# Layer 3 of a four-layer convolution and attention kernel: gate chain moved by a slot, two copies moved to ScalarE, copy order changed, lead-in rearranged

## The chip, the cores and the metric

The kernel runs on one core of a Trainium2 chip. The core has a matrix engine (PE in the profile; the loading of its stationary operand is the row PEld), a vector engine (DVE, VectorE), an activation engine (ACT, ScalarE), a general engine (POOL, GpSimd) and an engine that only issues DMAs and waits (SP, SyncE). Each engine works through its own list of instructions in order; where one needs what another makes, it waits on a semaphore. The metric is device time in microseconds of one execution; lower is better. Three executions of the kernel before took 3566.73, 3568.6 and 3573.8 us; their median, 3568.6, is the time before.

## What is computed

The input is 4 images of 256 channels and 48 x 48 pixels, f32. Four layers follow, each of the form `x = x + layer(gn(x))`, where `gn` is a group norm over groups of 8 channels. Layer 0 is attention with 8 heads, layer 1 a set of depthwise convolutions that make a gate, layer 2 attention with one head of 64 channels and a batch norm behind it, layer 3 a channel gate, a 3 x 3 depthwise convolution and an instance norm. The change touches the end of layer 2 and layer 3:

```python
def _L2_conv_ref(...):                       # x: 4 x 256 x 48 x 48, normalised
    ...
    y = jnp.einsum('bnm,bmc->bnc', attn, g_x)
    y = y.transpose(0, 2, 1).reshape(b, -1, h, w)
    wy = jnp.einsum('oc,bchw->bohw', W_w, y) + W_b[:, None, None]
    mean = wy.mean(axis=(0, 2, 3))
    var = wy.var(axis=(0, 2, 3))
    out = bn_gamma[:, None, None] * (wy - mean[:, None, None]) * jax.lax.rsqrt(var[:, None, None] + EPS) + bn_beta[:, None, None]
    return out

def _L3_conv_ref(x, attn_w1, attn_w2, refine_w, refine_b):
    ...
    p = jnp.mean(xw, axis=(2, 3))
    h = jax.nn.leaky_relu(p @ attn_w1.T, SLOPE)
    a = jax.nn.sigmoid(h @ attn_w2.T)
    y = xw * a[:, :, None, None]
    y = jax.lax.conv_general_dilated(y, refine_w, window_strides=(1, 1), padding='SAME', feature_group_count=C, dimension_numbers=('NCHW', 'OIHW', 'NCHW'))
    y = y + refine_b[None, :, None, None]
    mu = jnp.mean(y, axis=(2, 3), keepdims=True)
    var = jnp.mean(jnp.square(y - mu), axis=(2, 3), keepdims=True)
    y = (y - mu) * jax.lax.rsqrt(var + EPS)
    return jax.nn.leaky_relu(y, SLOPE)
```

The batch norm of layer 2 takes its mean and variance over all four images, so layer 3 can start only when the last image's attention is done.

## The kernel before

Layers 0 to 2 are one long stream in which attention slots are filled with the projections, norms and gates of other images. A table of jobs (`fills`, `due`) says in which slot each job is put into the engines' lists. The last phase is layer 2's attention of image 3: 27 slots, three units of 9. When a unit ends, `last` (line 429) schedules its denominator (`total_here`), the sum and division on VectorE (`fold`, `divide`) and `note`, two reductions of the denominator that feed a check of the number range.

Behind the attention come `sample_means` (bn_aggr for each image), `w_stats` of the last third of image 3 (line 1341: the product with W_w and bn_stats of it), and then layer 3's lead-in, lines 1405 to 1743: the batch norm's scale `sc2` and shift `bi2`, the images' means, the first products `first` and `ahead`, and for tiles 0 and 1 the steps `grow`, `border`, `spread_out` and `square`.

Layer 3 works on 8 tiles: image (in the order 1, 2, 3, 0) by half of the channels. Tile i has its padded picture in one of four buffers `pads` (50 x 50). `grow` (line 1457, VectorE) writes x plus layer 2's output into the picture, `border` (POOL) its rim. The depthwise convolution runs on PE. For this the picture is copied into `shifted`, a buffer with four sections j, each holding 32 channels' picture at up to three positions q of the partitions, shifted by one column. These copies are made by `spread_out(i, h)` for each half h of the picture: 12 copies of 32 x 1298 f32, of which 8 change partitions (q != j) and 4 don't. The 8 are DMAs on SP's queue. The 4 are POOL copies for h = 0 and DMAs on SP's queue for h = 1. There are three `shifted` buffers, used in turn.

The steady part is a table `events` of time slots (lines 1746 to 1812). A slot is one sixth of a tile: 12 matmuls (24 passes) of the convolution. Tile i starts at slot t = 6 i. In a slot the jobs are put out by rank: FRONT, CONV, PRODUCT, GROW, EVICT, SMALL, MOMENTS, SQUARE, SCALE, LAST, PLACE, STORE. So each engine's order is fixed by slot and then by rank; within one rank, by the order in which the jobs were entered, tile by tile. The jobs of a tile that starts at t:

- the picture is made at t-9 to t-7: W_w product on PE (PRODUCT, one PSUM tile `w` for all), `grow` on DVE, `border` at t-9; squares of it on ACT at t-8 to t-6; `spread_out` at t-6 (h = 0) and t-3 (h = 1)
- convolution at t to t+5; eviction and squares of the result on ACT at t+2 to t+7
- `moments` and `scales` on DVE at FRONT of t+8, with a power on POOL; `shift` on DVE at LAST of t+8
- normalising: `scale` on ACT at t+9 to t+11, `leak` and `gain` on DVE (LAST) at t+10 to t+12, `store` (DMA on SP) at t+11 to t+13.

For every second tile, that is for every image, the gate chain runs (class `Chain`, line 1513): `total` (DVE), `groups` (PE), `inverse` (DVE, POOL), `pooled` (DVE), `first_layer` (PE), `hidden` (DVE), `second_layer` (PE), `gate` (ACT), `scaled` (DVE). Its products land in free columns of the PSUM tile of the slot in which they are put out, `now["ps"]`. It is entered at t+1, each DVE or ACT step at FRONT of its slot and each PE step at SMALL. Twelve slots, two tiles, are one image's period. A similar chain of one matmul, `judge`, is entered at slot 8.

Of the kernel before, what the change touches and what calls it, by code (L numbers as in the profile page):

```python
# [78 lines left out]
def usual_path(  # L79
# [333 lines left out]

    due, fills = {}, {}

# [13 lines left out]
    def last(u, t):  # L429

        take(u)
        if u.get("soon"):
            todo = [
                (fills, 1, lambda: total_here(u)), (due, 2, lambda: fold(u, nc.vector)),
                (due, 2, lambda: divide(u, nc.vector)), (due, 2, lambda: note(u)),
            ]
            after = 3
        else:
            todo = [
                (fills, AT_TOTAL, lambda: total(u)), (due, AT_FOLD, lambda: fold(u, nc.gpsimd)),  # L440
                (due, AT_INVERT, lambda: invert(u)),
                (due, AT_DIVIDE, lambda: divide(u, nc.gpsimd)),
            ]
            after = AT_AFTER
        todo += [(fills, after, fn) for fn in u["after"]]
        for when, dt, fn in todo:
            when.setdefault(t + dt, []).append(fn)
# [623 lines left out]

    def w_mul(b, k, c):

        ab = [pj_tile()[:, :SL] for _ in range(2)]
        for i, cc in enumerate(HALVES):
            for r, out in zip(HALVES, ab):
                c0 = k * P + i * D
                nc.tensor.matmul(
                    out[cc], lhsT=Ww[r, c0 : c0 + D],
                    rhs=y_of(b)[r, c * SL : (c + 1) * SL], start=True, stop=True,  # L1080
                )
        return [(c, ab[0]), (c + L2C, ab[1])]

    def w_stats(b, k, c):
        for s, ps in w_mul(b, k, c):
            nc.vector.bn_stats(bst[:, k, b * NSL + s, :], ps)

    def l2_unit(b, c, s2):
        return {
            "pt": {}, "qc": slice(c * SL, (c + 1) * SL), "of": s2, "after": [],  # L1090
            "paired": PAIRED if b == B - 1 else range(NG), "scale": D ** -0.5,
            "soon": b == B - 1,
            "o": lambda: y_of(b)[:, c * SL : (c + 1) * SL],
        }
# [200 lines left out]
    for b in range(B):  # L1295
# [21 lines left out]
        else:  # L1317
            spread(work, stats(b, 0), [16, 17])
            spread(work, stats(b, 1), [23, 24])
            others.append((tap_matrices(), 1 + len(SHIFT), 4, 22))  # L1320
        phases.append(([l2_unit(b, c, twos[b]) for c in range(L2C)], work, others))
# [16 lines left out]
    attend(phases)  # L1338
    for b in range(NX):
        sample_means(b)  # L1340
    for k in range(NK):
        w_stats(B - 1, k, L2C - 1)
    strict.close()
# [60 lines left out]

    for sh in shifted:
        nc.gpsimd.memset(sh[0:32, 2:4, :], 0.0)
    first = [w_product(0, c, cv_tile()) for c in range(L2C)]
    ahead = [w_product(1, 0, w_tile())]

    mv2 = lp.tile([P, NK, 2], F32, name="mv2")  # L1410
    for k in range(NK):
        nc.vector.bn_aggr(mv2[:, k, :], bst[:, k].rearrange("p s f -> p (s f)"))
    sc2 = lp.tile([P, NK], F32, name="sc2")
    var2 = lp.tile([P, NK], F32, name="var2")
    nc.vector.tensor_scalar(var2, mv2[:, :, 1], BN_EPS, None, ALU.add)
    rsqrt(sc2, var2)
    bi2 = lp.tile([P, NK], F32, name="bi2")
    nc.vector.tensor_add(bi2, mv2[:, :, 0], vec[:, V_WB, :])
    nc.vector.tensor_sub(bi2, vec[:, V_WB, :], bi2)
    sample_means(B - 1)  # L1420
    nc.vector.tensor_mul(sc2, sc2, vec[:, V_G2, :])
# [15 lines left out]

    of_groups = columns_of(first[0], B * NK)
    nc.tensor.matmul(
# [16 lines left out]

    def grow(i, c, ps):

        n, k = TILES[i]
        xs = XT[SEQ[n]][:, k, :].rearrange("p (h r c) -> p h r c", h=2, c=HW)  # L1460
        to = inside(i, c)
        for h in range(2):
            nc.vector.scalar_tensor_tensor(
                to[:, h], ps[:, h, :SL].rearrange("p (r c) -> p r c", c=HW),
                sc2[:, k : k + 1], xs[:, h, c * RS : (c + 1) * RS, :], ALU.mult, ALU.add,
            )
# [28 lines left out]

    def place(i, h, j, q, eng):
        to = shifted[(2 * i + h) % 3][32 * q : 32 * q + 32, j, :CL]
        c0 = h * HB * W2 + SHIFT[j, q]
        fr = pads[i % 4][32 * j : 32 * j + 32, c0 : c0 + CL]
        if eng is nc.gpsimd:  # L1500
            eng.tensor_copy(to, fr)
        else:
            eng.dma_start(to, fr)

    def spread_out(i, h, own=None):

        for j, q in SHIFT:
            if q != j:
                place(i, h, j, q, nc.sync)
        for j in range(4):  # L1510
            place(i, h, j, j, own or (nc.sync if h else nc.gpsimd))

    class Chain:
# [5 lines left out]
        def steps(self):  # L1519
            of, b = {}, self.b  # L1520

            def total(_):
                of["sq"] = sq = small.tile([P, NK], F32, tag="gn_sq", name="gn_sq")
# [4 lines left out]

            def groups(ps):
                of["ps"] = ps[:, 0:NK]  # L1530
                nc.tensor.matmul(of["ps"], lhsT=gmat, rhs=of["sq"], start=True, stop=True)

            def inverse(_):
                gv = small.tile([P, NK], F32, tag="gn_gv", name="gn_gv")
                nc.vector.tensor_scalar(gv, of["ps"], GN_EPS, None, ALU.add)
                of["rs"] = small.tile([P, NK], F32, tag="gn_rs", name="gn_rs", bufs=6)
                rsqrt(of["rs"], gv)

            def pooled(_):
                of["pm"] = pm = small.tile([P, NK], F32, tag="pm", name="pm")  # L1540
                nc.vector.tensor_mul(pm, dev[:, b, :], of["rs"])

            def first_layer(ps):
                of["ps"] = ps[0:D, 0:1]
                for k in range(NK):
# [4 lines left out]

            def hidden(_):
                raw = small.tile([D, 1], F32, tag="hraw", name="hraw")
                nc.vector.tensor_copy(raw, of["ps"])
                of["hl"] = hl = small.tile([D, 1], F32, tag="hl", name="hl")
                nc.vector.scalar_tensor_tensor(hl, raw, SLOPE, raw, ALU.mult, ALU.max)

            def second_layer(ps):
                of["ps"] = ps[:, 0:NK]
                for k in range(NK):
                    nc.tensor.matmul(  # L1560
                        ps[:, k : k + 1], lhsT=w2[:, k * P : (k + 1) * P], rhs=of["hl"],
                        start=True, stop=True,
                    )

            def gate(_):
                of["ga"] = small.tile([P, NK], F32, tag="ga", name="ga")
                nc.scalar.activation(of["ga"], of["ps"], AF.Exp, scale=-1.0)

            def scaled(_):
                ga = of["ga"]  # L1570
# [6 lines left out]

            return [
                (total, groups), (inverse, None), (pooled, first_layer), (hidden, second_layer),
                (gate, scaled),  # L1580
            ]
# [122 lines left out]
    def judge():  # L1704

        of = {}

        def lows(_):
            ok = lp.tile([P, 2, LW], F32, name="ok")
# [4 lines left out]

        def count(ps):
            of["ps"] = ps[0:1, 0:1]
            nc.tensor.matmul(of["ps"], lhsT=of["okm"], rhs=ones[:, 0:1], start=True, stop=True)

        def compare(_):
            nc.vector.tensor_scalar(sound, of["ps"], P - 0.5, None, ALU.is_ge)  # L1720

        return [(lows, count), (compare, None)]

# [3 lines left out]

    grow(0, 0, first[0])
    edges()
    border(0)  # L1730
    for c in range(1, L2C):
        grow(0, c, first[c])
    for h in range(2):
        spread_out(0, h, nc.scalar)
    centres()
# [9 lines left out]

    FRONT, CONV, PRODUCT, GROW, EVICT, SMALL, MOMENTS, SQUARE, SCALE, LAST, PLACE, STORE = range(12)
    events = {}
# [6 lines left out]
    def put_chain(t, parts):  # L1754
        for dt, (head, tail) in enumerate(parts):
            at(t + dt, FRONT, lambda fn=head: fn(None))
            if tail:
                at(t + dt, SMALL, lambda fn=tail: fn(now["ps"]))

# [13 lines left out]
    def put_tile(t, cv, final):  # L1773
# [11 lines left out]
        at(t + 8, FRONT, cv.scales)  # L1785
        at(t + 8, LAST, cv.shift)
        for g in range(NG3):
            at(t + 9 + g, SCALE, lambda g=g: cv.scale(g))
            at(t + 10 + g, LAST, lambda g=g: cv.leak(g))
            at(t + 10 + g, LAST, lambda g=g: cv.gain(g))  # L1790
            at(t + 11 + g, STORE, lambda g=g: cv.store(g))

    def reload(k):
        nc.sync.dma_start(XT[0][:, k, :], x_out[:, k, :])

    for i, cv in enumerate(convs):
        t = i * NSL
# [6 lines left out]
        if i % NK == 0:  # L1804
            put_chain(t + 1, chains[i // NK].steps())
        if i < NK:
            at(t + 14, STORE, lambda k=cv.k: reload(k))
    put_chain(8, judge())
    T = len(convs) * NSL
    for t in range(max(T, max(events) + 1)):  # L1810
# [859 lines left out]
```

## Time and profile before

| what | us |
|---|---|
| median of three runs | 3568.6 |
| profiled execution, device time | 3567.38 |
| its span, first to last instruction | 3565.7 |
| layer 2's attention of image 3 ends (last `av` matmul) | about 3364.6 |
| first convolution matmul of layer 3 | 3389.13 |
| last convolution matmul ends | about 3547 |
| last instruction on data (DVE) | 3560.56 |

The profile was taken on one execution, whose device time is 1.7 us more than its span; times inside it are microseconds from the span's start. PE is busy for 96% of the whole span and its granted clock is 0.987 of full on average. Layer 3 with its lead-in is the last 200 us, and the change acts there and in the last 70 us of layer 2, so the views have to be read for these stretches alone; shares over the whole span say little about them.

### The profile page before, as it was taken

The numbers are of one execution on the slowest core, as the hardware profiler recorded it, in microseconds if no ns is written. First come the engines' busy times: TensorE is split into PE (matmuls) and PEld (weight loads), VectorE is DVE, ScalarE is ACT, GpSimd is POOL, SyncE is SP. The second block draws the span as 40 slices with busy tenths as digits, with TensorE's granted clock in tenths as the row PEclk, the third lists the DMA queues.
The fourth block names the chain that finished last, engine by engine and source line by source line (L and its number), as shares of the span: only waits on it lengthen the run. The fifth ranks groups of instructions, "written<-read, shape, count | busy, mean of one in ns | idle before, by whom it ended". The sixth has DMA issues, their size and how long they took to land. (4 is left out here: it accounts for less than half of the span.)

```text
span 3565.7 us, 88371 instructions
## 1 busy us (share of the span) xinstructions
PE 3436.9 (96%) x37036; PEld 1729.2 (48%) x37036; DVE 2554.7 (72%) x3472; ACT 2345.1 (66%) x3814; POOL 805.9 (23%) x615
## 2 busy tenths in 40 slices
PE   7999999999999999999999999999999999899886
PEld 4554555554444444444444444444444445565422
DVE  3455555567788788787887886878878878665856
ACT  4666666665886796658867965589678755555354
POOL 2333333321111010101001010111000126665432
PEclk9999999999999999999999999999999999999988
DMA  2211111111111111221111111111111100000087
GB/s 89 53 26 22 22 26 25 22 26 22 22 26 22 26 22 26 57 44 22 26 21 26 22 26 21 26 21 26 22 22 21 23 7 6 6 7 6 9 236 200
DMA packets 123575, 122.92 MB, mean 34 GB/s; under 512 B 59440, under 2 KB 113312, under 8 KB 122400
## 3 DMA queue, kind: packets, MB, share of 16 engines
q1 hardware_dynamic: 119456, 113.66, 16.6%
q8 instruction: 292, 4.78, 0.6%
q10 hardware_dynamic: 3712, 3.53, 0.4%
q14 instruction: 115, 0.94, 0.1%
HBM read 56.99 MB, written 11.80 MB: 19 GB/s over the span
## 5 line engine op out<-in xcount | busy, mean ns | idle before, releaser
L298 ACT ACTIVATE pt<-sc 128x768 f32<-128x768 f32 x1944 | 1475.2, 811 | 731.1 <-PE sc L292 722.9
L338 DVE TENSOR_TENSOR acc<-acc,pt 128x768 f32<-128x768 f32 x1368 | 1364.6, 997 | 173.1 <-ACT pt L298 72.8
L312 PE MATMUL av<-pt,v 64*64 64x384 f32 x13824 | 1274.8, 484 | 0.0
L292 PE MATMUL sc<-q,k 64*64 64x384 f32 x13824 | 1270.1, 482 | 0.8 <-ACT pt L298 0.8
L292 PEld LDWEIGHTS sc<-q,k 64*64 64x64 f32 x13824 | 525.2, 133 | 590.2 <-issue 543.1
L312 PEld LDWEIGHTS av<-pt,v 64*64 64x64 f32 x13824 | 518.1, 133 | 598.9 <-issue 565.9
L393 POOL TENSOR_TENSOR o<-o,rinv 128x384 f32<-128x384 f32 x95 | 120.8, 1271 | 1739.1 <-DMA rinv<-rinv 1730.0
L323 POOL TENSOR_TENSOR half<-pt 128x768 f32<-128x768 f32 x189 | 364.3, 1931 | 535.5 <-ACT pt L298 489.9
L338 DVE TENSOR_TENSOR acc<-acc,half 128x768 f32<-128x768 f32 x171 | 192.4, 1125 | 235.8 <-POOL half L323 234.8
L672 DVE SCALAR_TENSOR_TENSOR x<-pj,bo,x 128x384 f32<-128x384 f32 x192 | 118.4, 617 | 309.5 <-PE pj L659 308.2
L848 ACT ACTIVATE prod<-pd,wt 128x256 f32<-128x256 f32 x486 | 337.2, 765 | 0.2
L576 PE MATMUL pj<-xs,w 128*128 128x384 f32 (+1 forms) x720 | 275.4, 505 | 0.0
L576 PEld LDWEIGHTS pj<-xs,w 128*128 128x128 f32 x720 | 124.1, 189 | 127.9 <-issue 38.9
L312 PE MATMUL av<-pt,qv 64*64 64x384 f32 x1728 | 176.5, 497 | 0.0
L292 PE MATMUL sc<-qv,kd 64*64 64x384 f32 x1728 | 171.7, 487 | 2.4 <-ACT pt L298 2.4
L871 DVE TENSOR_REDUCE prod<-prod 128x256 f32<-128x1280 f32 x114 | 168.7, 1480 | 0.3 <-ACT prod L848 0.3
L659 PE MATMUL pj<-o,wo 128*128 128x384 f32 (+1 forms) x384 | 159.8, 499 | 5.7 <-issue 3.6
L607 PEld LDWEIGHTS pj<-w,xs 128*128 128x128 f32 x1080 | 134.5, 191 | 24.1 <-issue 1.2
L332 DVE TENSOR_TENSOR acc<-pt 128x768 f32<-128x768 f32 x99 | 119.9, 1212 | 26.6 <-ACT pt L298 26.6
L607 PE MATMUL pj<-w,xs 128*128 128x128 f32 x1080 | 134.9, 275 | 0.0
L389 POOL TENSOR_TENSOR o<-raw 128x384 f32<-128x384 f32 x95 | 121.0, 1273 | 44.6 <-ACT raw L385 44.6
L1604 PE MATMUL cv<-sh,taps 96*32 96x384 f32 (+1 forms) x1152 | 111.9, 524 | 10.0 <-DMA sh<-pad 8.6
(236 smaller groups left out, 2342.1 us busy)
## 6 DMA issues: line engine op xcount, KB each, us to landing
xs<-in_x_dram SPq DMA_DIRECT2D x90, 384.0 KB
sh<-pad SPq DMA_DIRECT2D x156, 162.2 KB
rinv<-rinv SPq DMA_DIRECT2D x208, 94.5 KB
out_dram<-x SPq DMA_DIRECT2D x24, 384.0 KB
l<-row SPq DMA_DIRECT2D x416, 1.5 KB
w<-in_wqkv_dram SPq DMA_DIRECT2D x32, 192.0 KB
x<-in_x_dram SPq DMA_DIRECT2D x4, 1152.0 KB
x<-in_x_dram SPq DMA_DIRECT2D x9, 384.0 KB
```

Source lines behind the costliest of these rows:

```text
L292: nc.tensor.matmul(ps[c * D : (c + 1) * D, h, :SL], lhsT=u["of"]["k"][r, j0 : j0 + D], rhs=u["of"]["q"][r, u["qc"]], start=True, stop=True,)
L298: nc.scalar.activation(pt, ps[:, :, :SL], AF.Exp, scale=u["scale"])
L312: nc.tensor.matmul(u["av"][h * D : (h + 1) * D, half, :SL], lhsT=value(u, j, h)[r], rhs=pt[r, h, :], start=j == 0, stop=j == JB - 1,)
L323: nc.gpsimd.tensor_add(half, pts[0], pts[1])
L338: nc.vector.tensor_add(u["acc"], u["acc"], term)
L389: eng.tensor_add(u["sum"], u["raw"][:, 0, :], u["raw"][:, 1, :])
L393: eng.tensor_mul(o, o, u["rinv"])
L576: nc.tensor.matmul(ps[:, :n], lhsT=at["w"][:, k, t, :], rhs=xs[s][:, k, :n], start=k == 0, stop=k == NK - 1,)
L607: nc.tensor.matmul(ps[:, i * P : (i + 1) * P], lhsT=xs[s][:, k, i * P : (i + 1) * P], rhs=at["w"][:, k, 2, :], start=k == 0, stop=k == NK - 1,
L659: nc.tensor.matmul(ps[:, :n], lhsT=wo[:, p, k * P : (k + 1) * P], rhs=o["o"][:, :n], start=True, stop=True,)
L848: nc.scalar.activation(bufs[n % 3][:, :, min(n, 1) + i].rearrange("p (r c) -> p r c", c=AS), pd[:, PAD + dr : PAD + dr + AS, PAD + dc : PA ...
L871: nc.vector.tensor_reduce(to, bufs[n % 3][:, :, : min(n, 1) + len(taps)], AX.X, ALU.add)
```

## The change

- `note` of the very last attention unit is no longer put out in the attention's slots but once at the end of the first part (`noted[0]()`).
- `sample_means` of images 0 to 2 move into slots 7, 10 and 15 of the last attention phase, and a new function `earlier(k)` computes mean and variance over images 0 to 2 in slots 18 and 21. After the attention only image 3 is added: some short DVE instructions take the place of two bn_aggr over all four images.
- The last `w_mul` writes to PSUM tiles of the scores (`wide=True`), so that both halves of the channels can be computed before one is read.
- The group means go to the columns of another of the `first` products; `grow` of tile 0 is done for the upper half first, and `spread_first` sends that half's 12 copies out before the lower half is grown. It uses SP for 6, ACT for 3, POOL for 2 and DVE for 1 (half 0), and SP for 8, ACT for 2, POOL for 2 (half 1). Two of three memsets of `shifted` come behind the first copies.
- In the steady part, the order of the 8 partition-changing copies alternates between low and high partitions (`AWAY`), and for h = 1 two of the four other copies are done by ACT instead of SP.
- The gate chain is entered at t+2 instead of t+1, has its own ranks (END, AFTER behind all others), takes one to two slots more, and its PSUM results are first copied by ACT (`read`) and then read by DVE. `judge` is changed in the same way.
- For the last tile but one, the three `scale` steps are put into one slot, and `leak`, `gain` and `store` a slot earlier for the last third.

```diff
         if u.get("soon"):
             todo = [
                 (fills, 1, lambda: total_here(u)), (due, 2, lambda: fold(u, nc.vector)),
-                (due, 2, lambda: divide(u, nc.vector)), (due, 2, lambda: note(u)),
+                (due, 2, lambda: divide(u, nc.vector)),
             ]
+            if u.get("final"):
+                noted.append(lambda: note(u))
+            else:
+                todo.append((due, 2, lambda: note(u)))
...
+    def earlier(k):
+
+        n = (B - 1) * NSL
+        nc.vector.bn_aggr(mv3[:, k, :], bst[:, k, :n].rearrange("p s f -> p (s f)"))
+        nc.vector.tensor_scalar(
+            var3[:, k : k + 1], mv3[:, k, 1:2], (B - 1) / B, BN_EPS, ALU.mult, ALU.add
+        )
...
+            spread(work, [lambda n=n: sample_means(n) for n in range(NX)], [7, 10, 15])
+            spread(work, [lambda k=k: earlier(k) for k in range(NK)], [18, 21])
...
-    for b in range(NX):
-        sample_means(b)
+    last_y = [w_mul(B - 1, k, L2C - 1, wide=True) for k in range(NK)]
     for k in range(NK):
-        w_stats(B - 1, k, L2C - 1)
+        for s, ps in last_y[k]:
+            nc.vector.bn_stats(bst[:, k, (B - 1) * NSL + s, :], ps)
+    sample_means(B - 1)
...
+    nc.vector.tensor_sub(step, mwy[:, B - 1, :, 0], mv3[:, :, 0])
+    nc.vector.tensor_mul(var2, step, step)
...
+    rsqrt(sc2, var2)
...
+    noted[0]()
     strict.close()
...
+    AWAY = [(0, 1), (2, 3), (0, 2), (2, 1), (1, 0), (3, 2), (1, 2), (3, 1)]
+
+    def spread_out(i, h):
+
+        for j, q in AWAY:
+            place(i, h, j, q, "sp")
         for j in range(4):
-            place(i, h, j, j, own or (nc.sync if h else nc.gpsimd))
+            place(i, h, j, j, ("sp", "act")[j % 2] if h else "pool")
+
+    def spread_first(h):
+
+        if h == 0:
+            how = dict(zip(AWAY, ("sp", "sp", "sp", "sp", "sp", "sp", "dve", "pool")))
+            how |= {(0, 0): "act", (1, 1): "act", (2, 2): "act", (3, 3): "pool"}
+        else:
+            how = dict.fromkeys(AWAY, "sp")
+            how |= {(0, 0): "act", (1, 1): "pool", (2, 2): "act", (3, 3): "pool"}
...
+            def read(p):
+                of["raw"] = small.tile([P, NK], F32, tag="chain", name="chain")
+                n = 1 if p < P else NK
+                nc.scalar.copy(of["raw"][0:p, 0:n], of["ps"])
+                return of["raw"][0:p, 0:n]
...
             return [
-                (total, groups), (inverse, None), (pooled, first_layer), (hidden, second_layer),
-                (gate, scaled),
+                (0, FRONT, total), (0, SMALL, groups),
+                (1, FRONT, lambda: read(P)), (1, END, inverse),
+                (2, END, pooled), (2, AFTER, first_layer),
+                (3, AFTER, lambda: read(D)), (4, FRONT, hidden), (4, SMALL, second_layer),
+                (5, FRONT, gate), (5, END, scaled),
             ]
...
-        return [(lows, count), (compare, None)]
+        return [(0, FRONT, lows), (1, SMALL, count), (2, FRONT, read), (2, END, compare)]
...
-    grow(0, 0, first[0])
+    for c in range(L2C - 1):
+        grow(0, c, first[c], [0])
     edges()
     border(0)
+    grow(0, L2C - 1, first[L2C - 1], [0])
+    grow(0, 0, first[0], [1])
+    spread_first(0)
+    for sh in shifted[1:]:
+        nc.gpsimd.memset(sh[0:32, 2:4, :], 0.0)
     for c in range(1, L2C):
-        grow(0, c, first[c])
-    for h in range(2):
-        spread_out(0, h, nc.scalar)
+        grow(0, c, first[c], [1])
+    spread_first(1)
...
+        soon = t + 2 * NSL == T
         for g in range(NG3):
-            at(t + 9 + g, SCALE, lambda g=g: cv.scale(g))
-            at(t + 10 + g, LAST, lambda g=g: cv.leak(g))
-            at(t + 10 + g, LAST, lambda g=g: cv.gain(g))
-            at(t + 11 + g, STORE, lambda g=g: cv.store(g))
+            at(t + 9 + (0 if soon else g), SCALE, lambda g=g: cv.scale(g))
+            dt = 10 + (min(g, 1) if soon else g)
+            at(t + dt, LAST, lambda g=g: cv.leak(g))
+            at(t + dt, LAST, lambda g=g: cv.gain(g))
+            at(t + dt + 1 - soon, STORE, lambda g=g: cv.store(g))
...
         if i % NK == 0:
-            put_chain(t + 1, chains[i // NK].steps())
+            put_chain(t + 2, chains[i // NK].steps())
```

## The prediction

> **What bounds the kernel now.** I read first the busy times by stage. Columns: length, then busy time of PE, PEld, DVE, ACT, POOL, then PE's clock, DMA share, GB/s.
>
> ```profile
> 3366.00:3397.00 31.00, 16.37 (x76) 3.79 (x72) 18.54 (x48) 3.98 (x8) 13.61 (x12) 0.60 0.40 92
> 3454.00:3473.00 19.00, 16.61 (x177) 5.39 (x177) 15.21 (x28) 11.03 (x22) 6.77 (x7) 0.91 0.86 243
> ```
>
> The lead-in leaves PE idle for half of its 31 us. In the steady part PE is the busiest engine, but not full; DVE comes next. Then who made PE wait from 3397 on (total us, times, longest):
>
> ```profile
> PE cv L1531 <- DVE gn_sq L1525: 15.2, 3, 5.1
> PE w L1398 <- DVE pad L1463: 4.5, 2, 2.4
> ```
>
> Both are DVE coming late. Waits for ACT (1.3) and for DMA (0.9) are small, so moving copies off SP is worth next to nothing in the steady part, although the DMA engines are 86% busy. The timelines of PE and of DVE show how it comes late (start, duration, line; brackets: idle before):
>
> ```profile
> 3430.36 0.88 PE L1398 MATMUL w<-y,Ww 64*64 64x384 f32 x8
> 3431.17 4.08 PE L1604 MATMUL cv<-sh,taps 96*32 96x384 f32 x48
> 3440.33 0.59 PE L1531 MATMUL cv<-gn_sq,gmat 128*128 128x2 f32 x2 [5.09 <-DVE gn_sq L1525]
> 3440.85 5.42 PE L1604 MATMUL cv<-sh,taps 96*32 96x384 f32 x48
> ...
> 3481.73 0.58 PE L1531 MATMUL cv<-gn_sq,gmat 128*128 128x2 f32 x2 [5.00 <-DVE gn_sq L1525]
> 3482.24 6.90 PE L1604 MATMUL cv<-sh,taps 96*32 96x384 f32 x48
> ```
>
> ```profile
> 3432.46 1.75 DVE L1687 SCALAR_TENSOR_TENSOR x<-x 128x768 f32<-128x768 f32 x1
> 3434.24 1.90 DVE L1692 SCALAR_TENSOR_TENSOR x<-pad,bi,x 128x768 f32<-128x768 f32 x1
> ...
> 3439.94 0.15 DVE L1524 TENSOR_REDUCE gn_sq<-ssq 128x2 f32<-128x6 f32 x1
> ...
> 3451.41 0.94 DVE L1687 SCALAR_TENSOR_TENSOR x<-x 128x768 f32<-128x768 f32 x1
> 3452.39 1.02 DVE L1692 SCALAR_TENSOR_TENSOR x<-pad,bi,x 128x768 f32<-128x768 f32 x1
> ```
>
> `total` (L1524) stands behind two pairs of `leak` and `gain`. A pair takes 1.96 us, but 3.65 (the second, left out here, 3.9) beside POOL's four copies:
>
> ```profile
> 3432.14 7.08 POOL L1501 COPY sh<-pad 32x1298 f32<-32x1298 f32 x4 [9.89 <-issue]
> ```
>
> So 9.1 us lie between the end of the last W_w product (3431.24, the zero of my count below) and `groups`, of which PE works 4. After the idle stretch 48 passes take 5.4 or 6.9 us instead of 4.08. The lead-in, from the timeline of all engines:
>
> ```profile
> 3370.28 0.42 DVE L395 TENSOR_SCALAR y<-y,bias 128x384 f32<-128x384 f32 x1
> ...
> 3383.73 16.33 SPq L1503 DMA_DIRECT2D sh<-pad  x17
> ...
> 3389.13 1.46 PE L1604 MATMUL cv<-sh,taps 96*32 96x384 f32 x2 [4.48 <-DMA sh<-pad]
> ...
> 3397.39 3.04 PE L1604 MATMUL cv<-sh,taps 128*32 128x384 f32 x24 [0.65 <-DMA sh<-pad]
> ```
>
> 13.0 us from the last y to the first copy, 13.7 more until all four sections j of the first half have landed.
>
> [...] Price of an ACT copy: [...] the trace has 0.92 to 0.94 for 768[...]. I take 1.37.
>
> **Lead-in.** (1) Behind the last y (3370.7) PE now computes both channel halves without waiting for bn_stats. At the slow clock 8 passes took 1.56 (L1398) to 2.0 us (L1078): ready at 3372.5 and about 3374.3, bn_stats (1.03) done at 3375.5, sample_means 0.48, four short instructions 0.75: 3376.7. POOL's power 0.72 ends at 3377.5, but DVE has by then three more and `note` (1.35) in front of it: 3378.5. Scale, shift and means 1.02 as before: 3379.6. Three `grow` halves and then one more at 0.55, `edges` 0.36, then the first copy: 3382.3 instead of 3383.7. Gain 1.4.
> (2) The work taken out of here, six bn_aggr of 0.2 and two new ones (between 0.24 for 36 elements and 0.80 for 144: 0.6 each) goes into the last attention phase, about 2.8 us of DVE. There DVE is at 17.1 of 21 us in 3345 to 3366, and PE already waited 1.58 and 1.08 for bst; I take 1 us lost, between 0 and 2.
> (3) Six DMAs instead of twelve stand before the first half. Before, three of them had landed at 5.3 us, four sections at 13.7; with some 20 copies of 166 KB in 13.7 us less 2 of latency one copy takes 0.6 to 0.66. Six: 2 + 6 x 0.66 = 6. ACT's three copies take 4.1, POOL's two 2.6 and DVE's one hides beside them. Convolution flows at 3382.3 + 6 = 3388.3; before, with a quarter of slot 0 already done, effectively at 3396.9.
> (4) Three slots at 2.04, 1.5 for the clock: 3395.9. Meanwhile ACT has five copies (6.9) and six squares (1.07 each): 3382.3 + 13.3 = 3395.6, total 0.35, groups and `read` 0.8: slot 3 starts at about 3397, with (2) at 3398. Before, 3404.6. Gain of all this 6.5 us; 3 if landings are as slow as before, 10 if the attention hides (2) and DVE does `note` while it waits.
>
> **First image's other slots.** No `leak` and `gain` yet; `first_layer` waits 1.5 for grow and pooled, and `read`, 0.4; `judge` a slot later loses its wait of 1.36. Zero.
>
> **Steady period (images 2 and 3 of the order).** Before: groups to groups 41.4 and 41.1 us. After, counting from the end of the product in slot 11:
> - slots 12 to 14 on PE: 6.1. DVE: the contended pairs end at 8.75, and in slot 14 tile by tile entry puts `moments` and `scales` (1.45) ahead of `total` (0.34): groups at 10.55. The extra slot hides 2.04, the queue takes back 1.45; the stall is 4.45 instead of 5.05.
> - groups 0.3; the next convolution writes the same PSUM tile and waits for ACT's `read`, as L1567 does now (0.42): 11.25.
> - slots 15, 16: 2 x (2.07 + 0.80) = 5.74: 17.0. `first_layer` is AFTER, and `pooled` END: behind grow (1.2) and an undisturbed pair (1.96) of slot 16. PE waits 3.4, works 0.33: 20.7. Before it went through without a wait.
> - slot 17: 2.87: 23.6. `hidden` is FRONT of slot 18 on DVE: behind grow 1.2 and a pair beside POOL, 3.7, itself 0.16: `second_layer` at 28.7, where PE was ready at 25.7; stall 3.0. It and the wait for `gate` 0.9: 29.6.
> - slots 19 to 23: 4.1 + 8.6 = 12.7: 42.3. The wait of 2.2 to 2.4 for pad (L1398) is gone, as PE is now late itself.
>
> Beside it the clock: before, 2.8 to 3.0 per period after stalls of 5 and 2.3; now three stalls of 4.5, 3.4 and 3.0; I take 4, between 1.3 (one stall at the least loss seen) and 6. Period 46.3 against 41.25: +5 each, +10 for both.
>
> **Last image.** No products, so DVE isn't held by PE: stall 4.45 and 0.8 of ACT reads against 5.09 and 0.26: zero. ACT's two copies per tile (2.7) fit in its free time (8.7 of 19 busy).
>
> **Tail.** Last but one tile's pair moves from behind the last tile to before its last bn_stats: 1.96 gained at the end, 1.96 lost at its start. Zero.
>
> **Sum** -6.5 + 10 = +3.5, taken as +4. On the profiled execution 3567.4 + 4 = 3571.4; the median of the runs is 1.2 above that one, so 3572.5.
>
> **Rivals.**
> A, the forecast (0.45): no change to be told, 0.2% (7 us) being what a measurement of this kernel can tell. Own range 3564 to 3576.
> B, slower (0.40): the ring PE product, grow, pair, pooled, `first_layer` is the bound, and three stalls keep the clock low. `hidden`[...] waits a POOL copy more (0.8), and the clock loses 5.5: period 48.6, +7.4 twice, with a lead-in of -5: +10, 3579. It decides once a period passes about 48. For it: `pooled` behind `gain` by rank; against: a slow PE hides part of DVE's time.
> C, faster (0.15): POOL's copies of slot 18 miss the pair of slot 17, so it takes 1.96, and one clock loss of 1.3 remains: 42.3 - 1.8 + 1.3 = 41.8, +0.6 twice, lead-in -9: -8, 3560.5. For it: ACT no longer waits for DVE's reads of PSUM (L1535 held its evictions 23.2 us); against: POOL's copies need only grow's first half.
>
> Range 3560 to 3585: C's edge, and B with a lead-in that gives 3 and one more clock loss per period. Chances: faster 0.15, same 0.45, slower 0.40.
>
> **What would show it.** Steps (1) to (4): copies from about 3383, full convolution from about 3389. Steady: PE waits at `first_layer` for DVE pm and at `second_layer` for DVE hl, about 3 us each in two images, with every later convolution queued behind them; groups stalls of 4 to 4.5; periods near 46. Wrong if those two waits are under 1 us, or if the period is below 42: then the answer is C.

## The result and the profile after

| what | before | after |
|---|---|---|
| median, us (10 executions each) | 3568.1 | 3580.0 |
| profiled execution, device time | 3567.38 | 3579.67 |
| its span | 3565.7 | 3577.9 |
| attention of image 3 ends | 3364.61 | 3368.08 |
| W_w product of slot 11 ends | 3431.24 | 3426.18 |
| W_w product of the next image's slot 11 ends | 3472.72 | 3476.80 |
| and of the third image's | 3513.71 | 3527.78 |
| last convolution matmul ends | 3547.11 | 3559.67 |

The change makes the kernel slower: ratio 1.0028, 95% interval 1.0019 to 1.0038. The forecast of 3572.5 was 7.5 us short, and of its cases it is B, "slower", that came, not A.

The fixed points of the table show where. A period is counted from the end of the W_w product of slot 11 to the end of the same product of the next image. From the end of the attention to the end of the first slot-11 product took 66.6 us and takes 58.1: the lead-in gains 8.5. The two steady periods took 41.5 and 41.0 and take 50.6 and 51.0: 19.1 lost. The last image gains 1.5, the tail 0.4. That is +8.7; the other 3.5 of the difference of the spans lie ahead of layer 3, and 2.8 of them ahead of all code that the change touches (the lag at the start of the last attention phase). The attention's end lies between 3364.0 and 3371.2 in the profiles of this study, though their code up to the last phase is the same, so layer 3 is read from its own fixed points below, and totals from medians.

The waits of PE in layer 3 after (us in all, times, longest); before, the first had 15.2 and the next two didn't exist:

```profile
PE cv L1585 <- DVE gn_sq L1579: 13.9, 3, 4.7
PE cv L1613 <- DVE hl L1608: 7.9, 2, 3.9
PE cv L1600 <- DVE pm L1595: 7.8, 3, 3.3
PE cv L1660 <- DMA sh<-pad: 2.1, 1, 2.1
```

Busy time by period, the columns as in the prediction, first of before and then of after:

```profile
3431.20:3472.65 41.45, 33.55 (x351) 11.65 (x347) 30.10 (x57) 22.40 (x44) 15.41 (x15) 0.92 0.84 235
3472.65:3513.60 40.95, 33.38 (x350) 11.70 (x346) 29.45 (x56) 20.66 (x40) 15.40 (x15) 0.92 0.89 243
```

```profile
3426.10:3476.70 50.60, 38.24 (x350) 14.24 (x346) 29.61 (x57) 30.36 (x54) 16.72 (x15) 0.83 0.75 210
3476.70:3527.70 51.00, 38.67 (x350) 14.21 (x346) 29.62 (x56) 28.23 (x50) 16.71 (x15) 0.83 0.60 167
```

The same 350 matmuls keep PE busy for 4.7 to 5.3 us more, because its clock fell from 0.92 to 0.83, and the idle rest grew from 7.9 to 12.4 (first period: 41.45 less 33.55, 50.60 less 38.24). So a period's loss is half waiting and half a slow clock. VectorE's work is the same, 29.6 us in 50.6: it has room, it only comes late. The timeline of PE after, in the first steady period:

```profile
3436.76 0.59 PE L1585 MATMUL cv<-gn_sq,gmat 128*128 128x2 f32 x2 [4.66 <-DVE gn_sq L1579]
3437.60 4.37 PE L1660 MATMUL cv<-sh,taps 96*32 96x384 f32 x24 [0.25 <-ACT chain L1573]
...
3449.42 0.39 PE L1600 MATMUL cv<-pm,w 128*64 128x1 f32 x4 [3.25 <-DVE pm L1595]
3449.74 3.83 PE L1660 MATMUL cv<-sh,taps 96*32 96x384 f32 x24
...
3460.39 1.01 PE L1613 MATMUL cv<-hl,w 64*128 64x1 f32 x4 [3.93 <-DVE hl L1608]
3461.66 8.57 PE L1660 MATMUL cv<-sh,taps 96*32 96x384 f32 x72 [0.26 <-ACT ga L1620]
```

A slot of 24 passes takes 2.14 at full rate, three take 6.01 (in the run warm below, clock 1.00). Behind each wait the convolution takes 1.7 to 2.6 longer than that; with the small products beside it the three waits cost 2.9, 1.7 and 3.0 us of slow clock. The clock itself shows how, the three half-rate stretches of this period and then, in the kernel before, those behind its waits of 5.09 and 5.00 (length, PE's busy time, clock, DMA share, GB/s):

```profile
3436.16:3442.99 6.83, 5.98 (x34) 0.50 0.76 224
3449.81:3453.23 3.42, 3.42 (x25) 0.50 0.39 139
3460.05:3466.88 6.83, 6.23 (x40) 0.50 0.65 185
```

```profile
3440.20:3443.62 3.42, 3.29 (x22) 0.50 0.61 226
3481.16:3487.99 6.83, 6.26 (x38) 0.50 0.93 250
```

In the traces of the kernels before and after each of the 27 stretches at 0.50 that end within the kernel is a whole multiple of 3.41 us, in the steady part one or two times that, and within a trace they all start whole multiples of 3.41 apart. In the other runs the clock that a steady period lost (1.00 less its clock, times its length) is within 0.2 us of a whole multiple of 1.71, the loss of 3.41 us at half rate: three times that in pooled_front's first (0.12 of 43.3), four in new_chain's first (0.14 of 49.2), none in warm's. So these waits are charged in clock steps, 3.41 us at half rate each: one costs half of what PE works in it, at most 1.7 us, and two at most 3.4. Nearly equal waits (5.09 and 5.00) cost one clock step and two. The steady periods of the kernel before have two clock steps each, those of the kernel after have five; in the first of these PE works 15.6 us at half rate, of which half, 7.8, is lost.

What VectorE did just before it gave `pm` (L1595) and `hl` (L1608):

```profile
3446.23 1.14 DVE L1495 SCALAR_TENSOR_TENSOR pad<-w,sc,x 128x384 f32<-128x384 f32 x2 [1.65 <-PE w L1442]
3447.29 0.95 DVE L1743 SCALAR_TENSOR_TENSOR x<-x 128x768 f32<-128x768 f32 x1
3448.28 1.02 DVE L1748 SCALAR_TENSOR_TENSOR x<-pad,bi,x 128x768 f32<-128x768 f32 x1
3449.21 0.15 DVE L1595 TENSOR_TENSOR pm<-dev,gn_rs 128x2 f32<-128x2 f32 x1
3454.45 1.14 DVE L1495 SCALAR_TENSOR_TENSOR pad<-w,sc,x 128x384 f32<-128x384 f32 x2 [5.09 <-PE w L1442]
3455.51 1.75 DVE L1743 SCALAR_TENSOR_TENSOR x<-x 128x768 f32<-128x768 f32 x1
3457.30 1.90 DVE L1748 SCALAR_TENSOR_TENSOR x<-pad,bi,x 128x768 f32<-128x768 f32 x1
3459.12 1.21 DVE L1608 SCALAR_TENSOR_TENSOR hl<-chain 64x1 f32<-64x1 f32 x1
```

`grow`, `leak` and `gain` stand in front of both. In the second case `leak`, `gain` and `hl` itself run while POOL copies (3455.19 to 3462.33), and `hl`, one column, takes 1.21 instead of 0.15 (the kernel before). VectorE itself stood idle for 5.09 us just ahead: it had waited for PE, which had waited for `pm`. This is the ring of rival B.

The lead-in after, from the timeline of all engines; before, the last y and the first copy stood at 3370.28 and 3383.73, and the convolution flowed from 3397.39:

```profile
3373.75 0.42 DVE L395 TENSOR_SCALAR y<-y,bias 128x384 f32<-128x384 f32 x1
...
3384.71 15.39 SPq L1533 DMA_DIRECT2D sh<-pad  x21
...
3389.21 10.02 PE L1660 MATMUL cv<-sh,taps 96*32 96x384 f32 x72 [2.11 <-DMA sh<-pad]
```

Of these 72 passes only two ran at 3389.21. The next weight load stands at 3390.66, behind 1.30 us of waiting for ScalarE's copies; from there the convolution flows, at half clock until 3395.2.

### The profile page after: what moved, and what is told of

The parts are those of the page before. It is cut to its first block, busy times and chain, and to the rows that moved or that the text cites. A ratio compares the mean times of both kernels' runs of the same rounds, so it can differ in the third digit from the quotient of the medians.

```text
span 3577.9 us, 88374 instructions
## 1 busy us (share of the span) xinstructions
PE 3446.2 (96%) x37036; PEld 1740.5 (49%) x37036; DVE 2557.5 (71%) x3475; ACT 2370.2 (66%) x3842; POOL 815.3 (23%) x619
```

## The experiments

All were timed beside the kernel before. "Ratio" is to that; medians of different rows are some 2 us uncertain (the kernel before had medians of 3567.6 to 3570.3 beside them). "Periods" are those of the two steady images, "last" is from the third slot-11 product to the last convolution matmul, in the profiled execution.

| kernel | median | ratio, 95% interval | periods | last |
|---|---|---|---|---|
| before | 3568.1 | | 41.5, 41.0 | 33.4 |
| after | 3580.0 | 1.0028 (1.0019 to 1.0038) | 50.6, 51.0 | 31.9 |
| old_chain | 3562.6 | 0.9982 (0.9976 to 0.9989) | 39.3, 39.8 | 33.5 |
| old_chain_copies | 3561.5 | 0.9976 (0.9966 to 0.9986) | 40.9, 38.9 | 33.0 |
| new_chain | 3587.9 | 1.0053 (1.0039 to 1.0067) | 49.2, 50.3 | 33.6 |
| warm | 3562.8 | 0.9981 (0.9972 to 0.9989) | 43.4, 43.3 | 30.6 |
| pooled_front | 3564.6 | 0.9984 (0.9976 to 0.9991) | 43.3, 44.0 | 33.2 |
| no_pool | 3560.6 | 0.9977 (0.9968 to 0.9987) | 40.2, 47.8 | 28.7 |
| two_moved | 3553.3 | 0.9951 (0.9937 to 0.9965) | 40.0, 38.3 | 33.5 |
| early | 3558.1 | 0.9974 (0.9962 to 0.9986) | 40.0, 40.2 | 32.8 |
| early2 | 3552.8 | 0.9950 (0.9936 to 0.9964) | 36.9, 37.4 | 34.8 |
| early3 | 3552.8 | 0.9947 (0.9934 to 0.9961) | 38.2, 37.4 | 32.1 |
| early4 | 3543.5 | 0.9930 (0.9916 to 0.9943) | 34.1, 41.1 | 26.4 |
| early4_sp | 3547.1 | 0.9938 (0.9924 to 0.9951) | 37.4, 41.1 | 28.4 |

### Which part of the change costs

old_chain: the kernel after with the chain's old steps, read from PSUM by VectorE as before, and the old `judge` (the lines below show the steps).

```diff
-                (0, FRONT, total), (0, SMALL, groups),
-                (1, FRONT, lambda: read(P)), (1, END, inverse),
-                (2, END, pooled), (2, AFTER, first_layer),
-                (3, AFTER, lambda: read(D)), (4, FRONT, hidden), (4, SMALL, second_layer),
-                (5, FRONT, gate), (5, END, scaled),
+                (0, FRONT, total), (0, SMALL, groups), (1, FRONT, inverse),
+                (2, FRONT, pooled), (2, SMALL, first_layer), (3, FRONT, hidden),
+                (3, SMALL, second_layer), (4, FRONT, gate), (4, FRONT, scaled),
...
-            put_chain(t + 2, chains[i // NK].steps())
+            put_chain(t + 1, chains[i // NK].steps())
```

> The changed kernel with the gate chain (and judge) of the kernel before: entered at t+1, old ranks, VectorE reads PSUM. All else of the change stays. Theory S (stalls): the loss is the chain's alone, three PE waits per image on VectorE steps that queue behind leak and gain, each with a slow clock after it. Then the periods from the W_w product of slot 11 to that of the next image fall from 50.6 and 51.0 us to 41 to 42, the lead-in's gain of 8.6 (end of attention to that product) stays, and the time is 3557 to 3563. Theory C (copies and start): the two ACT copies per tile (ACT busy 22 to 30 us per period) and the other DMA order, or the phase in which the shorter lead-in starts the steady part, make the periods long. Then they stay above 46 and the time is above 3568.

It gave 3562.6 and periods of 39.3 and 39.8, shorter than the 41 to 42 expected. new_chain is the opposite, the kernel before with only the new steps:

> The kernel before with the new gate chain (and judge) alone: t+2, END and AFTER, ACT reads. Theory S: periods of about 50.5 to 51 with waits of PE near 4.6 (gn_sq), 3.3 (pm) and 3.9 (hl); before plus 19 for two images less 1.5 in the last one: 3583 to 3588. Theory C: periods of 41 to 44 and a time of 3567 to 3573.

It gave 3587.9, and the same three waits as the kernel after, to the tenth (the second line is the old lead-in's):

```profile
PE cv L1537 <- DVE gn_sq L1531: 13.9, 3, 4.7
PE cv L1612 <- DMA sh<-pad: 8.6, 4, 4.5
PE cv L1565 <- DVE hl L1560: 7.9, 2, 3.9
PE cv L1552 <- DVE pm L1547: 7.8, 3, 3.3
```

Both ways round, the chain takes some 17 to 20 us (3580.0 less 3562.6; 3587.9 less 3568.1) and the rest gives some 6 to 8. Theory C falls. Old_chain is already faster than the kernel before.

old_chain_copies also puts the steady part's copies back:

```diff
-        for j, q in AWAY:
-            place(i, h, j, q, "sp")
+        for j, q in SHIFT:
+            if q != j:
+                place(i, h, j, q, "sp")
         for j in range(4):
-            place(i, h, j, j, ("sp", "act")[j % 2] if h else "pool")
+            place(i, h, j, j, "sp" if h else "pool")
```

> The 'old_chain' kernel with the steady part's copies as in the kernel before, too: the old order, and all eight plus four of h = 1 on SP. What is left of the change is the lead-in and the tail. Old_chain had periods of 39.4 and 39.8 where before had 41.4 and 41.1. If the copies made that (alternation, or two copies off SP), the periods go back to 41 to 41.5 and the time is 3 to 4 more: 3565.5. If they are worth nothing, as my prediction had it, it stays within 1 of old_chain's 3562.6.

3561.5, and two periods of 79.7 together against 79.1: order and engine of these copies are worth nothing that can be told at this length of period. Its two periods are 2.8 shorter than those of before (82.5). In the traces that is PE's wait for `pad`, 3.3 in all instead of 4.5, and three clock steps instead of four (PE busy for 65.4 instead of 66.9). What is left of the change in it is the lead-in and the tail; why `pad` then comes sooner isn't settled. The lead-in's own parts were not tried one by one: what each gives is read from the trace alone.

### What a wait costs

warm: the kernel after with throw-away matmuls in the gaps.

```diff
+            def busy(count):
+                for _ in range(count):
+                    nc.tensor.matmul(
+                        now["ps"][:, 8:128], lhsT=gmat, rhs=gmat[:, 0:120], start=True, stop=True
+                    )
             def groups():
+                busy(20 if self.n else 0)
...
             def first_layer():
+                busy(14 if self.n in (1, 2) else 0)
...
             def second_layer():
+                busy(17 if self.n in (1, 2) else 0)
```

> The changed kernel with extra matmuls whose products nobody reads (gmat by 120 of its own columns, about 0.21 us each) on PE just before the chain's steps: 20 before groups (images 2 to 4 of the order), 14 before first_layer and 17 before second_layer (images 2 and 3). They fill the waits of 4.6, 3.3 and 3.9 us almost whole, and take nothing else away. If idleness sets the slow clock, and that is half of the loss, the convolution after each wait runs at full rate, the 38.2 us in which PE is busy per period come down to 30.4 and the time is some 8 less per period: 14 to 17 less in all, 3563 to 3567. If the waits alone are the loss, with the slow clock from something else (load, power), PE stays slow and the time is 3578 to 3584.

It gave 3562.8, 17 less than after, though PE runs 51 matmuls (102 passes) more in each steady period, and `groups` comes no earlier behind the slot-11 product than in the kernel after (10.60 against 10.58):

```profile
3422.80:3466.10 43.30, 42.79 (x451) 23.34 (x451) 29.48 (x57) 28.22 (x50) 16.73 (x15) 1.00 0.82 226
3466.10:3509.40 43.30, 42.79 (x456) 23.45 (x452) 29.51 (x56) 28.00 (x50) 16.72 (x15) 1.00 0.80 218
```

The clock is at 1.00 throughout and each period is 7.3 to 7.7 shorter. That is the price of the slow clock alone, and idleness is what brings it: filled with work, the same waits leave no half-rate stretch in either period. Without the throw-away passes (4.72, 3.38 and 4.05 us in the timeline, 0.24 a matmul where 0.21 was expected) PE is busy for 30.6 us.

pooled_front: one word.

```diff
-                (2, END, pooled), (2, AFTER, first_layer),
+                (2, FRONT, pooled), (2, AFTER, first_layer),
```

> The changed kernel with one word changed: pooled at FRONT of its slot instead of END, so ahead of grow, leak and gain on VectorE. My step for first_layer (PE waits there for pooled behind grow and a pair): the wait of 3.25 us goes in both steady images, with about 1.7 of slow clock behind it; each period 4 to 5 shorter: 3570 to 3573. Rival, that VectorE as a whole sets the period: the same time comes back in front of hl, which then waits longer than 3.9, and the time is 3578 or more.

3564.6: 5 better than the expected 3570 to 3573. Its first period:

```profile
3429.80:3473.10 43.30, 34.20 (x350) 13.16 (x354) 29.68 (x57) 29.63 (x52) 16.73 (x15) 0.88 0.85 239
```

The wait for `pm` is gone, and 4.0 us of PE's busy time with it (38.24 to 34.20), not 1.7; the waits for `gn_sq` and `hl` are as long as before to 0.05 us. So VectorE had room. The clock's losses don't simply add up wait by wait: in both periods the same wait of 3.93 for `hl` brought one clock step here and two in the kernel after.

two_moved takes out the wait for `hl` too (VectorE itself reads the product for `hidden`):

```diff
-                (2, END, pooled), (2, AFTER, first_layer),
-                (3, AFTER, lambda: read(D)), (4, FRONT, hidden), (4, SMALL, second_layer),
+                (2, FRONT, pooled), (3, SMALL, first_layer),
+                (3, SCALE, hidden), (4, SMALL, second_layer),
```

> 'pooled_front' with hidden moved too: first_layer in the next (odd) slot, hidden right behind it and before that slot's leak and gain, read by VectorE. total and groups stay. Of the change's three waits only that for gn_sq (4.6) is left. If each wait costs itself and the slow clock after it, and VectorE as a whole has room, the wait of 3.93 for hl goes with 1.4 to 1.7 of clock: periods 43.3 and 44.0 fall to 37.5 to 39, time 3552 to 3556. Rival: VectorE late as a whole: waits for pad or gn_sq grow, time 3560 or more.

3553.3 as expected, and periods of 40.0 and 38.3, the first 1.0 above the expected span; waits of 1.2 and 0.8 for `pad` are new. With these two waits gone the kernel is 27 us faster than after: they and the clock behind them are more than the whole loss.

no_pool: `... if h else "pool"` becomes `... if h else "sp"`.

> The changed kernel, but the four copies per tile that POOL makes in the steady part (h = 0, q = j) are DMAs on SP. Theory S with the contention as the cause of VectorE's lateness: every leak and gain pair takes 1.96 us instead of 3.7 to 3.9, PE's wait for gn_sq falls from 4.6 to about 1.1, that for hl from 3.9 to about 2.2, that for pm stays near 3.3, about 2.5 of clock loss go too: period 43, last image 4 less, time about 3560. Rival: with 22 instead of 18 DMAs per tile the DMA engines (share 0.75 of a period now) become the bound, PE waits for sh, periods 47 or more, time 3572 or more.

3560.6, as expected. The waits fell to 1.0 (gn_sq) and 1.2 (hl), and stayed at 3.26 (pm). VectorE's groups in the first steady period, after and then no_pool (busy us, mean ns):

```profile
L1748 DVE SCALAR_TENSOR_TENSOR x<-pad,bi,x 128x768 f32<-128x768 f32 x7 | 10.7, 1524 | 0.2
L1743 DVE SCALAR_TENSOR_TENSOR x<-x 128x768 f32<-128x768 f32 x6 | 8.3, 1391 | 0.0
```

```profile
L1748 DVE SCALAR_TENSOR_TENSOR x<-pad,bi,x 128x768 f32<-128x768 f32 x7 | 7.1, 1019 | 0.2
L1743 DVE SCALAR_TENSOR_TENSOR x<-x 128x768 f32<-128x768 f32 x6 | 5.7, 946 | 0.0
```

POOL's eight copies per period cost VectorE 7.3 us (29.6 busy against 22.3). The rival was half right: with 22 DMAs per tile one wait of 6.7 us for a transfer (the profile names a store, `out_dram`) came up in the second period, which took 47.8.

### A version without the waits

early keeps the copies and moves four steps:

```diff
-                (0, FRONT, total), (0, SMALL, groups),
-                (1, FRONT, lambda: read(P)), (1, END, inverse),
-                (2, END, pooled), (2, AFTER, first_layer),
-                (3, AFTER, lambda: read(D)), (4, FRONT, hidden), (4, SMALL, second_layer),
+                (-2, SCALE, total), (0, SMALL, groups),
+                (1, FRONT, lambda: read(P)), (1, FRONT, inverse),
+                (2, FRONT, pooled), (2, SMALL, first_layer),
+                (3, FRONT, lambda: read(D)), (3, FRONT, hidden), (4, SMALL, second_layer),
```

> The changed kernel with other places for four steps of the chain on VectorE: total in slot t, before that slot's leak and gain instead of behind them two slots later; inverse, pooled and hidden at FRONT, first_layer at SMALL of the same slot, second_layer where it was. ACT still reads. Theory S: the three waits fall under 1.2 us each, the clock stays near 1, periods 33 to 37, last image 4 to 6 less: 3542 to 3552. Rival: VectorE (30 us of work per period) is late as a whole, so the wait only moves to the W_w product or to another step: periods 40 or more, time 3559 or more.

3558.1, missed by 6. The old waits went, a new one came, PE first and then ScalarE:

```profile
3438.66 0.39 PE L1600 MATMUL cv<-pm,w 128*64 128x1 f32 x4
3444.09 3.54 PE L1660 MATMUL cv<-sh,taps 96*32 96x384 f32 x24 [5.04 <-ACT chain L1573]
```

```profile
3438.54 2.57 ACT L1535 COPY sh<-pad 32x1298 f32<-32x1298 f32 x2
...
3443.90 0.14 ACT L1573 COPY chain<-cv 64x1 f32<-64x1 f32 x1
```

The product sits in the even slot's half of a PSUM tile. The next slot's convolution writes the other half and waits for the read that was put out ahead of it, which stands on ScalarE behind the two new copies and three longer instructions. early2 therefore makes the products in odd slots and lets VectorE read for `hidden` (the new steps; the last line of the old list stays):

```diff
+                (-2, SCALE, total), (1, SMALL, groups),
+                (2, FRONT, lambda: read(P)), (2, FRONT, inverse), (2, FRONT, pooled),
+                (3, SMALL, first_layer), (3, SCALE, hidden), (4, SMALL, second_layer),
```

> As 'early', but the PSUM products that the next convolution writes beside are made in odd slots, so that the convolution doesn't wait for a read of them: groups a slot later, first_layer a slot later with hidden right behind it on VectorE, which reads PSUM itself. Theory Q (the 5.0, 2.3 and 2.6 us in 'early' are PE waiting for ScalarE's read, late in its queue behind two copies): these waits go, periods 36 to 37.5, last image 3 less: 3546 to 3551. Rival D: the DMA engines (0.82 to 0.88 busy in 'early', so 33 to 35 us per period) or VectorE are next and the periods stay at 39 or more: 3555 or more.

3552.8, 1.8 above the expected range: periods as expected, but the last image lost 2.0 where 3 were to be gained. VectorE now stood at `inverse` behind the same read, and PE for it:

```profile
3515.18 0.58 PE L1600 MATMUL cv<-pm,w 128*64 128x1 f32 x4 [5.19 <-DVE pm L1595]
```

early3 has VectorE read there, too: `(1, SMALL, groups), (1, SQUARE, inverse), (2, FRONT, pooled)`.

> 'early2' with inverse read from PSUM by VectorE right behind groups, in the same slot, so ScalarE reads nothing for the chain but the gate. Theory Q (in 'early2' VectorE stands 3.7 to 4.8 us at inverse because ScalarE's read is queued behind its two copies, and PE then waits 2.9 for pad and in the last image 5.2 for pm): these waits go, periods 35 to 37, last image 3 to 5 less, time 3544 to 3549. Rival D: DMA, 0.97 busy in the second period of 'early2', holds the periods at 37, and ScalarE's eviction now waits for VectorE's read: 3550 to 3556.

3552.8, a miss. The time is in rival D's range, but PE's waits say otherwise: 2.8 us for a DMA, 10.6 in three waits for ScalarE's gate. It is the same trap once more, at the last thing that ScalarE reads:

```profile
3443.56 0.60 PE L1614 MATMUL cv<-hl,w 64*128 64x1 f32 x4
3448.35 8.46 PE L1660 MATMUL cv<-sh,taps 96*32 96x384 f32 x72 [4.19 <-ACT ga L1621]
```

early4 puts the gate behind its slot's convolution:

```diff
-                (5, FRONT, gate), (5, END, scaled),
+                (5, EVICT, gate), (5, END, scaled),
```

> 'early3' with the gate put out behind its slot's convolution (EVICT) instead of ahead of it (FRONT). In 'early3' PE waited 4.2, 2.1 and 4.3 us for ScalarE's gate, because second_layer writes the PSUM tile that the next slot's convolution also writes. Theory Q (a step on a loaded engine costs PE only where a later convolution is made to wait for it): these waits and their 2.5, 1.7 and 1.8 us of slow clock go, periods 33 to 36, last image 30: 3538 to 3544. Rival D: DMA holds the periods at 37, only the last image gains: 3545 to 3549.

3543.5, 0.7% under the kernel before. Its two periods and the last image:

```profile
3419.80:3453.90 34.10, 30.89 (x350) 11.81 (x354) 28.76 (x58) 26.94 (x46) 16.10 (x15) 1.00 0.82 234
3453.90:3495.00 41.10, 33.53 (x352) 12.81 (x354) 28.34 (x57) 26.75 (x46) 16.09 (x15) 0.88 0.97 268
3495.00:3521.40 26.40, 25.56 (x300) 13.41 (x298) 19.11 (x49) 20.15 (x36) 8.06 (x7) 1.00 0.74 215
```

The first period and the last image run at a clock of 1.00; in the second one DMA is at 0.97 and one wait for a transfer (again a store by the profile) takes 6.3, with three clock steps behind it. Rival D was right for that one period. early4_sp gives the two ScalarE copies back to SP:

> 'early4' with all four unmoved copies of h = 1 on SP again, none on ScalarE (20 instead of 18 DMAs per tile). With periods of 41 to 50 us these two copies made no difference. If DMA is the next limit once PE's waits are gone (0.83 to 0.97 busy in 'early2'), the periods are 1 to 3 longer than in 'early4' with waits of PE for sh, time 2 to 6 more. If ScalarE's queue is the next limit, it is 1 to 4 less.

3547.1, as expected if DMA is the next limit. The difference lies in the first period, 3.2 longer, where PE waits 3.3 for `sh` (1.9 for a transfer in early4), and in the last image, 2.0 longer with a wait of 1.2. The second period keeps its length, though DMA is busy for the whole of it and the wait, now for `sh`, takes 6.9:

```profile
3423.80:3461.10 37.30, 32.77 (x350) 12.60 (x351) 29.24 (x58) 22.82 (x45) 16.79 (x15) 0.95 0.87 238
3461.10:3502.20 41.10, 32.86 (x354) 12.37 (x354) 29.30 (x57) 20.54 (x40) 16.78 (x15) 0.92 1.00 272
```

## Why the prediction was right and wrong

The forecast was case A, no change to be told; what came was B, which the text gave 0.40. B had named the ring, the three waits and the extra price of `hidden` beside POOL; A's sum of +3.5 came out at +9.4 because the clock's term was too small by 3.6 us in each of two periods and that of `second_layer` by 0.9, of which the lead-in and the last image took back only a part. By its own steps:

- **(1) y to the first copy.** Forecast 11.6, measured 10.5 (3374.17 to 3384.71), 13.0 before.
- **(2) Attention.** 1 taken, between 0 and 2. Over the last phase the lag behind the kernel before grew from 2.81 to 3.47, so 0.7.
- **(3) First copy to full convolution.** Forecast 6; the first two passes came after 4.5, the flow after 5.95 (3390.66). The 2 us of latency in that sum were an estimate without a line: in the trace of before the DMA engines are at work 1.3 us after the first issue (share 0.06 from 3383.73 to 3385.0, then 0.99 to 3388.0). In the kernel after the first of SP's six copies landed 2.9 us after its issue (3384.71 to 3387.61), the other five 0.67 to 0.80 apart, the last after 6.5. ScalarE's copy took 1.27 (20.4 for 16), not my 1.37; that was an estimate, which in the trace of before rests on 0.93 for 768 elements and 0.84 ns for each further one (its copies of 384 and 768, L612 and L385, take 0.48 and 0.80). The clock stayed at half for longer than assumed: the three slots ended 14.5 after the first copy, where 13.6 were forecast.
- **(4) Lead-in in all.** Forecast a gain of 6.5. From the attention's end to the slot-11 product it was 8.5 (66.6 to 58.1); less the 0.7 of (2), 7.8.
- **First image's other slots: zero.** Right: `first_layer` waited 1.3 there, in a stretch whose gain is in the line above.
- **Steady, groups.** Forecast 10.55 after the slot-11 product with a wait of 4.45; measured 10.58 (3436.76 less 3426.18) and 4.66.
- **Steady, first_layer.** Wait forecast 3.4, measured 3.25.
- **Steady, second_layer.** Wait forecast 3.0, measured 3.93. Missing was what B had: `hidden` itself among POOL's copies, 1.21 instead of 0.16.
- **Steady, the clock: the step that failed.** "I take 4, between 1.3 ... and 6". Measured 7.3 to 7.7 per period (warm), 38.24 busy against 30.6. The 4 is little more than the 2.8 to 3.0 lost in a period before, though three long waits now stood where one of 5 and one of 2.3 had been, and the text gives no reason for it. Each wait was charged anew: between two waits PE had two slots and their products to do (7 to 9 us) and was back at full rate in the second (2.14). Five clock steps came in a period where the kernel before had two. 46.3, and 3.6 more of clock, and 0.9 of `second_layer`, is 50.8; measured 50.6 and 51.0. Both rival B's price (5.5) and the upper bound were short as well.
- **Last image and tail: zero.** -1.5 and -0.4. The wait for groups was 4.61 against 5.09, and less clock went behind it (48 passes in 5.69 instead of 6.84: one clock step instead of two).
- **Copies in the steady part: nothing.** Right as long as the period is 40 us (old_chain against old_chain_copies). Not right without PE's waits: early4 against early4_sp is 3.7 us.

In the traces: 0.7 for (2), -8.5 behind it, 19.1, -1.5 and -0.4 make +9.4, against a forecast of +3.5. The medians differ by 11.9, the profiled executions by 12.3. The rest lies ahead of the last attention phase, in code that the change doesn't touch; the attention's end moves by more than that between executions, and how much of it is chance in the medians isn't settled.

The range held because it was wide and, in part by luck, because the two errors, 9 on two periods and -3 on the rest, partly cancel.

B's place and point of decision were right ("once a period passes about 48"), its sizes not: +9.6 for each of two periods, where it had +7.4, and -8 for the lead-in, where it had -5. That its 3579 is so near the measured 3580.0 is these two errors cancelling, and the part ahead of the last phase.

C had spoken of POOL's copies missing the pair. They didn't in the kernel after; no_pool, where every pair is clear of them, is 19 us faster.

## What to carry to other kernels

Here a step of the side chain that stood behind other work in one engine's queue cost PE time where something on PE was made to wait for it: the gate, late on ScalarE, held PE for 10.6 us in early3, and for none in early4, where only its place relative to the convolution had changed. So put such a step ahead of the long instructions of its slot, and put what needs it behind the main work. Where one PSUM tile held both the small product and the main one, a read of the small product, put out ahead of the next main matmul, was a wait of PE (5.04 us in early, 4.19 in early3): look for it on every engine that reads, as here it went from VectorE to ScalarE's read and to the gate. A wait of PE is to be priced with the clock behind it, here 1.7 to 3.0 us for 3 to 5 us of idleness, once for each of the three.

## What the runs showed of the hardware

- Waits of PE of 4.66, 3.25 and 3.93 (kernel after) were each followed by work at half rate, and so was one of 1.17 in no_pool (three slots behind it in 7.71 instead of 6.01), while one of 1.08 there was not (6.01). A wait's length alone doesn't tell: 5.09 and 5.00 in the kernel before, and 3.93 in the kernel after and in pooled_front, cost one clock step (3.41 us at half rate) in one place and two in the other. What decides between one and two wasn't tested.
- Work that nobody needs shortened the kernel: 102 more passes made each period 7.3 to 7.7 us shorter, since they kept the clock at 1.00.
- A VectorE instruction on one or two columns took 1.21 and 1.03 us beside POOL's copies (`hl` in the kernel after, `gn_sq` in early), 0.15 to 0.16 without: small steps can pay POOL's price as well as large ones. Not all did: beside the same copies a reduction of one input just ahead of that `gn_sq` (L1578) took 0.15; in the lead-in of the kernel after, beside POOL's first two copies, two steps of two inputs (L1485, L1486) took 0.16 each and two halves of `grow`, which reads PSUM, 1.15 together, where one half without copies took 0.61.
